# A two-layer decoder on one core: attention outputs scaled in place by transposed reciprocals

## The chip, the cores and the metric

The kernel is one program on 1 core of a Trainium2 chip. The metric is the device time in microseconds (us). Engines are named as the profile names them: PE (matmuls, with PEld for its weight loads), DVE (vector), ACT (activations), POOL (GpSimd) and SP (DMA issues).

## The reference

The input x is 64 batches x 128 tokens x 256 features, float32; ctx has the same shape. Six blocks follow one another, each added to x:

```python
x = x + mamba(layernorm(x))                       # state space scan
x = x + attention16(layernorm(x), ctx, ctx)       # 16 heads of 16, rotary, output projection
x = x + recurrence(layernorm(x))                  # 64 steps over the batches, gated, tanh output
x = x + self_attention(rmsnorm(x) * g)            # 16 query heads, 4 key heads, s + s @ w_o
x = x + wide_attention(layernorm(x), ctx, ctx)    # one head of 256
x = x + experts(layernorm(x))                     # top 2 of 8, and a shared expert
```

The change lies in the two 16-head attentions. For each head of 16 features they are

```python
attn_w = softmax(q @ k.T * scale, axis=-1)        # 1/4 in the cross attention, 1/16 in the self attention
out = attn_w @ v                                  # 128 tokens x 16 features a head
```

The cross attention ends with `out @ Wo + bo`; the self attention adds both `s` and `s @ w_o` to x.

## The kernel before

Four batches make a group of T = 512 tokens (G = 4), and there are NG = 16 groups. x stays in 16 tiles `X[g]`. There are four stages, one after the other: mamba; "work2" with the cross attention and the recurrence; "work3" with the self attention, the wide attention and the routing; and the experts, who work on rows that the routing has scattered to memory (`xs`). The text calls them stages 1 to 4.

Within a stage the work is written as generators, and `run(tasks)` sets their order: every generator has a turn at which it starts, and in each turn every active one advances to its next `yield`. In stages 2 and 3 the inputs of group g start at turn 16g, its recurrence at 16g + 42, its wide attention and routing (`cross_and_route`) at 16g + 43. The attention of batch b is two units, c = 0 and 1, of 8 heads each, that start at turn 16g + 16 + 4b + 2c: one unit every two turns, 8 units a group, 128 a stage, 256 in all. Each engine then executes its own instructions in the order in which they were issued; a scheduler fills in the semaphore waits. [...]

One unit, `heads`:

- POOL builds `kbd` (L284), the keys of four heads on a block diagonal, and PE multiplies the queries with it into `s` (L236; a float32 matmul is two records in the profile).
- DVE takes the maximum of every row and head (L241) and multiplies it with -scale (L242).
- ACT computes eight exponentials, one a head, with that maximum as bias (L245), into one tile `e`.
- PE transposes the eight (L250) into one tile `pt`; ACT copies the first half of it to `eT` (L252) and DVE the second (L253).
- PE multiplies `eT` with the values (L261) into `av`. The tile `v` has 16 columns of values and 16 of ones for each head, so that `av` has the weighted values in 16 rows and the sum of the exponentials in 16 others.

After the second unit of a batch ACT copies `av` (L267), PE transposes it with four transposes (`pa`, L272), DVE takes the reciprocals of the sums (L275) and multiplies the values with them (L277); two more transposes (`po`, L291, in `rows_T`) and an ACT copy (L293) bring the result back into the form that the output projection wants (L557 in the cross attention, L698 in the self attention). DVE adds that to x (L560, L701). The self attention has POOL add the outputs themselves to x (L690). POOL fills the columns of ones with a MEMSET for every batch (L533) or group (L669).

What stands around it: `norm` (bn statistics on DVE, L172; a power on POOL, L163; the scaling on DVE, L189) and `transposed` (PE, `pt_ln`, L200; ACT L202, DVE L204) before each projection (L211, L219); the rotary products (L512, L514, L519); the recurrence (L593, L598); the wide attention's exponentials, which are written with `accum_out` (L741), so that ACT also reads out the sum of a row with an instruction of its own; the routing's scatters by POOL (L842), eight for each group, of rows `xnr`. The first units of stage 3 are fed through a single tile `xo` that SP loads and POOL and ACT prepare (L643 to L645).

## Time and profile before

| | |
|---|---|
| Runs, us | 3532.44, 3531.86, 3532.04: median 3532.04 |
| The profiled execution | 3483.77 us, its span 3482.0 us |
| Stage 1 | 0 to about 787 us |
| Stage 2 | to about 1990; the last unit's maximum at 1924 |
| Stage 3 | to about 3075; the last unit's maximum at 2981, the last L701 at 3000.8 |
| Stage 4 | to the end |
| PE, DVE, ACT, POOL busy | 3176.3, 2273.2, 1471.3, 1302.8 us |
| L245, exponentials | 2048, 383 ns each |
| L241, maxima / L242, their scaling | 256 of 1213 ns / 256 of 333 ns |
| L250, transposes of e | 2048, 302 ns each from issue to end |
| mean granted clock of TensorE | 0.948 |

Times within a profile are microseconds from the start of its span. A group's row in the profile gives its busy time in all, the mean of one in ns, and after the bar the idle time of the engine just before these instructions with what ended most of it. Busy time is the union of records that overlap, so that a mean can be longer than the distance from one instruction to the next.

### The profile page before, as it was taken

How to read it: one execution, taken by the hardware profiler on the slowest of the kernel's cores; microseconds unless marked ns; L12 is line 12 of the kernel's file. 1: busy time of each engine (PE TensorE's matmuls, PEld its weight loads, DVE VectorE, ACT ScalarE, POOL GpSimd, SP SyncE). 2: the span in 40 equal slices, each digit the busy share in tenths (PEclk: the TensorE clock that was granted, in tenths of full speed). 3: DMA queues.
4: the chain of work that ended last, by engine and by line, in shares of the span. 5: the costliest groups of instructions: out<-in, count | busy, mean ns of one | idle time of the engine just before them, and what ended most of it. 6: DMA issues, size and time to landing. Idle time of an engine off the chain costs nothing.

```text
span 3482.0 us, 48744 instructions
## 1 busy us (share of the span) xinstructions
PE 3176.3 (91%) x17486; PEld 2033.9 (58%) x17486; DVE 2273.2 (65%) x5498; ACT 1471.3 (42%) x3781; POOL 1302.8 (37%) x1290
## 2 busy tenths in 40 slices
PE   7899999998999999999999767999999999779989
PEld 4555555554666666666666633556566655468845
DVE  7999889965565556655565344777777777543355
ACT  3333333334545555455545234555555555213301
POOL 2444444455332323332332064233333333223276
PEclk9999999999999999999999878999998999789999
DMA  9980000001000000000000011101010101157655
GB/s 312 343 283 1 1 1 1 1 14 30 13 19 13 19 13 13 14 18 19 13 13 7 34 50 41 37 32 42 32 43 32 42 31 43 60 167 227 200 182 180
DMA packets 170658, 229.48 MB, mean 66 GB/s; under 512 B 19504, under 2 KB 142896, under 8 KB 170416
## 3 DMA queue, kind: packets, MB, share of 16 engines
q1 hardware_dynamic: 152448, 180.19, 16.0%
q0 software_dynamic: 17968, 46.18, 4.3%
q8 instruction: 138, 2.26, 0.3%
q14 instruction: 104, 0.85, 0.1%
HBM read 113.71 MB, written 127.93 MB: 69 GB/s over the span
## 4 chain that ended last, share of the span: by engine, by line
PE 62%; DVE 24%; POOL 6%; ACT 4%; DMA 2%; issue 2%; ACTq 0%; DVEq 0%; POOLq 0%; SPq 0%
PE proj L211 17%; PE pt L250 7%; PE s L236 6%; PE pu L593 5%; DVE acc L333 4%; DVE xn L189 4%; PE pgu L1019 4%; PE pv L219 3%; PE pt_ln L200 2%; PE av L261 2%; DVE mx L241 2%; PE pd L1028 2%; PE pxo L219 2%; PE pd L1079 1%; PE po L439 1%
## 5 line engine op out<-in xcount | busy, mean ns | idle before, releaser
L245 ACT ACTIVATE e<-s,mx 128x128 f32<-128x128 f32 x2048 | 555.9, 383 | 479.6 <-DVE mx L242 390.0
L284 POOL TENSOR_TENSOR kbd<-kT,consts 128x512 f32<-128x512 f32 x192 | 202.9, 1057 | 682.3 <-PE s L236 674.0
L253 DVE COPY eT<-pt 128x512 f32<-128x512 f32 x256 | 176.0, 687 | 392.7 <-ACT eT L252 391.7
L250 PE MATMUL pt<-consts,e 128*128 128x128 f32 x2048 | 362.5, 302 | 64.4 <-ACT e L245 62.6
L250 PEld LDWEIGHTS pt<-consts,e 128*128 128x128 f32 x2048 | 258.5, 148 | 180.8 <-ACT e L245 124.5
L211 PE MATMUL proj<-xnT,win 128*128 128x512 f32 x640 | 308.1, 621 | 48.9 <-DVE xc L323 45.0
L241 DVE TENSOR_REDUCE mx<-s 128x8 f32<-128x1024 f32 x256 | 310.5, 1213 | 10.0 <-PE s L236 9.9
L236 PE MATMUL s<-kbd,qT 64*128 64x512 f32 x1024 | 311.1, 686 | 1.5 <-POOL kbd L284 1.5
L252 ACT COPY eT<-pt 128x512 f32<-128x512 f32 x256 | 153.0, 598 | 191.7 <-PE pt L250 190.5
L211 PEld LDWEIGHTS proj<-xnT,win 128*128 128x128 f32 x640 | 119.9, 197 | 192.6 <-issue 112.6
L842 POOL DMA_INDIRECT xs<-xnr,r_rows x128 | 126.6, 989 | 271.5 <-DMA xs<-xnr,r_rows 183.8
L333 DVE SCALAR_TENSOR_TENSOR acc<-proj,convw,acc 128x508 f32<-128x508 f32 (+2 forms) x288 | 209.2, 730 | 7.7 <-ACT acc L329 6.2
L593 PEld LDWEIGHTS pu<-c,fu 128*128 128x128 f32 x1536 | 184.8, 196 | 24.9 <-issue 18.9
L593 PE MATMUL pu<-c,fu 128*128 128x128 f32 x1536 | 187.4, 280 | 8.9 <-DVE c L609 8.9
L392 POOL TENSOR_TENSOR ua<-consts,dt 128x1024 f32<-128x1024 f32 x64 | 121.9, 1906 | 179.7 <-DVE dt L366 150.6
L261 PE MATMUL av<-eT,v 128*32 128x128 f32 (+1 forms) x3072 | 174.5, 328 | 10.0 <-DVE eT L253 9.8
L211 PE MATMUL proj<-xnT,fx 128*128 128x512 f32 x384 | 173.4, 601 | 10.1 <-DVE v L534 9.6
L200 PE MATMUL pt_ln<-consts,xn 128*128 128x128 f32 x640 | 125.6, 316 | 61.5 <-DVE xn L189 39.5
L163 POOL TENSOR_TENSOR ln_rstd<-ln_ve,neghalf 128x4 f32<-128x4 f32 x96 | 98.0, 1021 | 210.4 <-DVE ln_ve L176 158.8
L189 DVE TENSOR_SCALAR xn<-x,ln_mv,ln_rstd 128x256 f32<-128x256 f32 x256 | 142.0, 600 | 40.4 <-POOL ln_rstd L163 40.4
L598 DVE TENSOR_TENSOR xg<-pu,xg 128x512 f32<-128x512 f32 (+1 forms) x128 | 71.4, 558 | 131.6 <-PE pu L593 131.6
L172 DVE BATCH_NORM_STATS2 ln_st<-x 128x6 f32<-128x256 f32 x384 | 146.3, 406 | 13.2 <-DMA x<-in_x_dram 6.2
(266 smaller groups left out, 6508.5 us busy)
## 6 DMA issues: line engine op xcount, KB each, us to landing
xs<-zeros SPq DMA_DIRECT2D x64, 1024.0 KB, 11.1
xs<-xs SPq DMA_DIRECT2D x71, 256.0 KB, 3.4
ys<-y SPq DMA_DIRECT2D x71, 256.0 KB, 2.3
ctxT<-in_ctxT_dram SPq DMA_DIRECT2D x32, 512.0 KB, 3.9
xo<-xo SPq DMA_DIRECT2D x32, 512.0 KB, 3.5
x<-in_x_dram SPq DMA_DIRECT2D x16, 512.0 KB, 8.9
xn<-xnT SPq DMA_DIRECT2D x16, 512.0 KB, 2.6
xnT<-xn SPq DMA_DIRECT2D x16, 512.0 KB, 4.6
```

The costliest lines, as they stand in the source:

```text
L189: nc.vector.tensor_scalar(xn[:, b, :], x[:, b, :], mv[:, b, 0:1], rstd[:, b:b + 1], ALU.subtract, ALU.mult)
L200: nc.tensor.transpose(pt[:, b * P:(b + 1) * P], xn[:, b, c * P:(c + 1) * P], ident)
L211: nc.tensor.matmul(o[:m, :], lhsT=w[:, k, m0:m0 + m], rhs=rhs[:, k, :], start=(k == 0), stop=(k == 1))
L236: nc.tensor.matmul(s[:, hf * 4:hf * 4 + 4, :], lhsT=q[rows], rhs=kb[rows, :, :], start=True, stop=True,)
L241: nc.vector.tensor_reduce(mx, s, AX.X, ALU.max)
L245: nc.scalar.activation(e[:, h, :], s[:, h, :], AF.Exp, bias=mx[:, h:h + 1], scale=scale)
L250: nc.tensor.transpose(pt[:, h, :], e[:, h, :], ident)
L253: nc.vector.tensor_copy(eT[:, 4:8, :], pt[:, 4:8, :])
L261: nc.tensor.matmul(av[j * 32:j * 32 + 32, place, :], lhsT=vals, rhs=eT[:, which, :], start=True, stop=True,)
L284: nc.gpsimd.tensor_tensor(out=kb, in0=mid(k, 4), in1=last(head, P), op=ALU.mult)
L333: nc.vector.scalar_tensor_tensor(acc[:, :, k:], pv[:, :, :P - k], convw[:, c, 3 - k:4 - k], acc[:, :, k:], ALU.mult, ALU.add,)
L593: nc.tensor.matmul(pu[:, i, :], lhsT=fu[:, k, c * P:(c + 1) * P], rhs=c2[:, k, :], start=(k == 0), stop=(k == 1),)
```

## The change

Nine edits, all in the two attentions and in what feeds them:

1. Tiles that two engines fill or that are read in halves become separate tiles: `xnT`, `qT` and `kT` of the cross attention, `e`, `eT`, `pt` (tags pt0 and pt1[...]), and `xg`.
2. The factor -scale moves into the queries: POOL multiplies `xwq` and `xbq` with -0.25 and `lwq` with -1/16 once, and ACT writes `ym`, `yu` and `ymb` of the wide attention with -1/16. DVE then takes the minimum, and the exponential has scale -1. L242 and its sister L737 go.
3. The exponentials of `heads` get an `accum_out` into `den`, 128 tokens x 16 heads.
4. Per batch DVE takes the reciprocal of `den`, an ACT copy spreads it to 16 columns a head (`rd`, 128x256), PE transposes that with two transposes (`prd`), and ACT copies them out (`prs`).
5. DVE multiplies the first two columns of tiles of `av`, as they lie in PSUM, with `prs` and has `oT`. The copy `avs`, the four transposes `pa`, L277, and the transposes `po` with their copy go.
6. The values lie in three (stage 3: two) lasting tiles, whose 32 columns from 16 to 48 are zero from the start: even and odd heads accumulate into the same 32 rows of `av`. The columns of ones and their MEMSETs go. In the self attention a unit has eight products of 128 columns in place of four of 256.
7. The self attention adds the identity to the diagonal blocks of `lwo` once, and POOL's L690 goes.
8. The tail of a batch has four yields fewer, and the recurrence and `cross_and_route` start four turns earlier, at 16g + 38 and 16g + 39.
9. The routing stores its transposed rows with two DMAs a group in place of one.

```diff
@@ -155,6 +155,8 @@
+    for w in (xwq, xbq):
+        nc.gpsimd.tensor_scalar_mul(w, w, -0.25)
...
@@ -193,23 +195,26 @@
     def transposed(work, ps, xn, bufs=2):
-        xnT = work.tile([P, 2, T], F32, tag="xnT", name="xnT", bufs=bufs)
+        xnT = [work.tile([P, T], F32, tag=f"xnT{c}", name=f"xnT{c}", bufs=bufs) for c in range(2)]
         for c in range(2):
             pt = ps.tile([P, T], F32, tag="mm", name="pt_ln")
             for b in range(G):
                 nc.tensor.transpose(pt[:, b * P:(b + 1) * P], xn[:, b, c * P:(c + 1) * P], ident)
             if c == 0:
-                nc.scalar.copy(xnT[:, c, :], pt)
+                nc.scalar.copy(xnT[c], pt)
             else:
-                nc.vector.tensor_copy(xnT[:, c, :], pt)
+                nc.vector.tensor_copy(xnT[c], pt)
         return xnT
+    def halves(t):
+        return [t[:, c, :] for c in range(2)]
...
@@ -237,61 +241,79 @@
                 s[:, hf * 4:hf * 4 + 4, :], lhsT=q[rows], rhs=kb[rows, :, :],
                 start=True, stop=True,
             )
         mx = work.tile([P, 8], F32, tag="mx", name="mx", bufs=2)
-        nc.vector.tensor_reduce(mx, s, AX.X, ALU.max)
-        nc.vector.tensor_scalar(mx, mx, -scale, None, ALU.mult)
-        e = work.tile([P, 8, P], F32, tag="e", name="e", bufs=2)
+        nc.vector.tensor_reduce(mx, s, AX.X, ALU.min)
+        e, eT = (
+            [work.tile([P, 4, P], F32, tag=f"{n}{i}", name=f"{n}{i}", bufs=2) for i in range(2)]
+            for n in ("e", "eT")
+        )
+        if c == 0:
+            state[b, "den"] = work.tile([P, 16], F32, tag="den", name="den", bufs=4)
+        den = state[b, "den"]
         for h in range(8):
-            nc.scalar.activation(e[:, h, :], s[:, h, :], AF.Exp, bias=mx[:, h:h + 1], scale=scale)
-        yield
-        yield
-        pt = ps.tile([P, 8, P], F32, tag="pt", name="pt")
-        for h in range(8):
-            nc.tensor.transpose(pt[:, h, :], e[:, h, :], ident)
-        eT = work.tile([P, 8, P], F32, tag="eT", name="eT", bufs=2)
-        nc.scalar.copy(eT[:, 0:4, :], pt[:, 0:4, :])
-        nc.vector.tensor_copy(eT[:, 4:8, :], pt[:, 4:8, :])
-        yield
+            nc.scalar.activation(
+                e[h // 4][:, h % 4, :], s[:, h, :], AF.Exp, bias=mx[:, h:h + 1], scale=-1.0,
+                accum_out=den[:, c * 8 + h:c * 8 + h + 1],
+            )
+        yield
+        yield
+        for i in range(2):
+            pt = ps.tile([P, 4, P], F32, tag=f"pt{i}", name=f"pt{i}")
+            for h in range(4):
+                nc.tensor.transpose(pt[:, h, :], e[i][:, h, :], ident)
+            if i == 0:
+                nc.scalar.copy(eT[i], pt)
+            else:
+                nc.vector.tensor_copy(eT[i], pt)
+        if c == 1:
+            nc.vector.reciprocal(den, den)
+            rd = work.tile([P, 16, 16], F32, tag="rd", name="rd", bufs=2)
+            nc.scalar.copy(rd, last(den, 16))
+        yield
+        if c == 1:
+            pr = ps.tile([P, T], F32, tag="mm", name="prd")
+            for k in range(2):
+                nc.tensor.transpose(
+                    pr[:, k * P:(k + 1) * P],
+                    rd[:, 8 * k:8 * k + 8, :].rearrange("p h e -> p (h e)"), ident,
+                )
+            prs = work.tile([P, 2, P], F32, tag="prs", name="prs", bufs=2)
+            nc.scalar.copy(prs.rearrange("p c t -> p (c t)"), pr[:, :D])
         yield
         if c == 0:
             state[b] = ps.tile([P, 4, P], F32, tag="av", name="av")
         av = state[b]
-        for vals, which, j, place in vh(c):
-            nc.tensor.matmul(
-                av[j * 32:j * 32 + 32, place, :], lhsT=vals, rhs=eT[:, which, :],
-                start=True, stop=True,
-            )
+        for odd in range(2):
+            for j in range(4):
+                h = 2 * j + odd
+                nc.tensor.matmul(
+                    av[j * 32:j * 32 + 32, c, :], lhsT=vh(h), rhs=eT[h // 4][:, h % 4, :],
+                    start=(odd == 0), stop=(odd == 1),
+                )
         if c == 1:
-            avs = work.tile([P, 4, P], F32, tag="avs", name="avs", bufs=2)
-            nc.scalar.copy(avs, av)
-            yield
-            yield
-            pa = ps.tile([P, T], F32, tag="mm", name="pa")
-            for g4 in range(4):
-                nc.tensor.transpose(pa[:, g4 * P:(g4 + 1) * P], avs[:, g4, :], ident)
-            pav = pa.rearrange("p (h e) -> p h e", e=32)
-            rd = work.tile([P, 16], F32, tag="rd", name="rd", bufs=2)
-            nc.vector.reciprocal(rd, pav[:, :, 16])
-            o = work.tile([P, D], F32, tag="o", name="o", bufs=2)
-            nc.vector.tensor_tensor(
-                o.rearrange("p (h e) -> p h e", e=16), pav[:, :, 0:16], last(rd, 16), ALU.mult
-            )
-            state[b] = o
+            yield
+            oT = work.tile([P, 2, P], F32, tag="oT", name="oT", bufs=2)
+            nc.vector.tensor_tensor(oT, av[:, 0:2, :], prs, ALU.mult)
+            state[b] = oT
+    def values_of(work, n, i):
+        v = work.tile([P, n, 64], F32, tag=f"v{i}", name=f"v{i}")
+        nc.gpsimd.memset(v[:, :, 16:48], 0.0)
+        return v
+    def pairs(v):
+        return v.rearrange("p n (f e) -> p n f e", e=16)[:, :, 0:4:3, :]
     def block_diagonal(work, k):
         kb = work.tile([P, 4, P], F32, tag="kbd", name="kbd", bufs=2)
         nc.gpsimd.tensor_tensor(out=kb, in0=mid(k, 4), in1=last(head, P), op=ALU.mult)
         return kb
-    def rows_T(work, ps, o):
-        po = ps.tile([P, T], F32, tag="mm", name="po")
-        for c in range(2):
-            nc.tensor.transpose(po[:, c * P:(c + 1) * P], o[:, c * P:(c + 1) * P], ident)
-        oT = work.tile([P, 2, P], F32, tag="oT", name="oT", bufs=2)
-        nc.scalar.copy(oT.rearrange("p c t -> p (c t)"), po[:, :D])
-        return oT
     XS = scratch.tile([8 * CAP + TS, D], F32, tag="xs", name="xs")
...
@@ -480,6 +502,10 @@
+        wd = lwo[:, c, c * P:(c + 1) * P]
+        nc.gpsimd.tensor_tensor(out=wd, in0=wd, in1=ident, op=ALU.add)
+    nc.gpsimd.tensor_scalar_mul(lwq, lwq, -1.0 / 16)
...
@@ -510,17 +536,17 @@
-                tv = t[:, c, :].rearrange("p (b t) -> p b t", b=G)
+                tv = ts[c].rearrange("p (b t) -> p b t", b=G)
-            got[g, tag] = t
-            yield
-            yield
-        got[g, "c"] = cT
+            got[g, tag] = ts
+            yield
+            yield
+        got[g, "c"] = halves(cT)
...
@@ -529,28 +555,21 @@
             if c == 0:
                 pv = ps.tile([P, T], F32, tag="mm", name="pv")
                 project_rows(pv[:, :D], got[g, "c"], xwv, b)
-                v = work.tile([P, 16, 32], F32, tag="v", name="v", bufs=3)
-                nc.gpsimd.memset(v[:, :, 16:32], 1.0)
+                v = got["v"][(g * G + b) % 3]
                 nc.vector.tensor_tensor(
-                    v[:, :, 0:16], pv[:, :D].rearrange("p (h e) -> p h e", e=16),
-                    xbv.rearrange("p (h e) -> p h e", e=16), ALU.add,
+                    pairs(v), pv[:, :D].rearrange("p (n f e) -> p n f e", f=2, e=16),
+                    xbv.rearrange("p (n f e) -> p n f e", f=2, e=16), ALU.add,
                 )
                 got[g, b, "v"] = v
             v = got[g, b, "v"]
-            return lambda c: [
-                (v[:, h, :], h % 8, h % 4, h // 4) for h in range(8 * c, 8 * c + 8)
-            ]
+            return lambda h: v[:, 4 * c + h // 2, h % 2 * 32:h % 2 * 32 + 32]
         yield from heads(
-            work, ps, b, c, got, got[g, "qT"][:, c, tb],
-            lambda: block_diagonal(work, got[g, "kT"][:, c, tb]), values, 0.25,
+            work, ps, b, c, got, got[g, "qT"][c][:, tb],
+            lambda: block_diagonal(work, got[g, "kT"][c][:, tb]), values,
         )
         if c == 1:
-            o = got[b]
-            yield
-            yield
-            oT = rows_T(work, ps, o)
-            yield
+            oT = got[b]
             yield
             pr = ps.tile([P, T], F32, tag="mm", name="pr")
             for k in range(2):
...
@@ -569,12 +588,14 @@
-        xg = work.tile([P, 6, T], F32, tag="xg", name="xg")
+        xgs = [work.tile([P, n, T], F32, tag=f"xg{n}", name=f"xg{n}") for n in (4, 2)]
-                nc.scalar.activation(xg[:, c, :], pp, AF.Identity, bias=fb[:, c:c + 1])
+                nc.scalar.activation(
+                    xgs[c // 4][:, c % 4, :], pp, AF.Identity, bias=fb[:, c:c + 1]
+                )
...
@@ -613,10 +633,10 @@
-        ps = PsumPool(psp, {"mm": 3, "s": 1, "pt": 1, "av": 1})
-        got = {"c2": c2}
+        ps = PsumPool(psp, {"mm": 3, "s": 1, "pt0": 1, "pt1": 1, "av": 1})
+        got = {"c2": c2, "v": [values_of(work, 8, i) for i in range(3)]}
-        tasks += [(16 * g + 42, recurrence(g, work, ps, got)) for g in range(NG)]
+        tasks += [(16 * g + 38, recurrence(g, work, ps, got)) for g in range(NG)]
...
@@ -665,9 +685,8 @@
-        v = work.tile([P, G * 4, 32], F32, tag="v", name="v", bufs=2)
-        nc.gpsimd.memset(v[:, :, 16:32], 1.0)
-        nc.scalar.copy(v[:, :, 0:16], pv[:, :D].rearrange("p (h e) -> p h e", e=16))
+        v = got["v"][g % 2]
+        nc.scalar.copy(pairs(v), pv[:, :D].rearrange("p (n f e) -> p n f e", f=2, e=16))
...
@@ -681,17 +700,10 @@
         yield from heads(
             work, ps, ("o", b), c, got, qT[:, c, tb], keys,
-            lambda: lambda c: [
-                (v[:, b * 4 + j, :], slice(j, 8, 4), j, slice(2 * c, 2 * c + 2)) for j in range(4)
-            ], 1.0 / 16,
+            lambda: lambda h: v[:, b * 2 + h % 4 // 2, h % 2 * 32:h % 2 * 32 + 32],
         )
         if c == 1:
-            o = got["o", b]
-            nc.gpsimd.tensor_tensor(out=X[g][:, b, :], in0=X[g][:, b, :], in1=o, op=ALU.add)
-            yield
-            yield
-            oT = rows_T(work, ps, o)
-            yield
+            oT = got["o", b]
             yield
             pr = ps.tile([P, T], F32, tag="mm", name="pr")
             for k in range(2):
...
@@ -727,19 +740,18 @@
-                    s[:, b, :], lhsT=qT[:, k, tb], rhs=cT[:, k, tb], start=(k == 0), stop=(k == 1)
+                    s[:, b, :], lhsT=qT[:, k, tb], rhs=cT[k][:, tb], start=(k == 0), stop=(k == 1)
-        nc.vector.tensor_reduce(mx, s, AX.X, ALU.max)
+        nc.vector.tensor_reduce(mx, s, AX.X, ALU.min)
-        nc.vector.tensor_tensor(mx, qb, mx, ALU.subtract)
-        nc.vector.tensor_scalar(mx, mx, 1.0 / 16, None, ALU.mult)
+        nc.vector.tensor_tensor(mx, mx, qb, ALU.subtract)
-                e[:, b, :], s[:, b, :], AF.Exp, bias=mx[:, b:b + 1], scale=1.0 / 16,
+                e[:, b, :], s[:, b, :], AF.Exp, bias=mx[:, b:b + 1], scale=-1.0,
...
@@ -779,7 +791,8 @@
-        nc.sync.dma_start(out=XN[g], in_=xnT)
+        for c in range(2):
+            nc.sync.dma_start(out=XN[g][:, c, :], in_=xnT[c])
...
@@ -849,7 +862,7 @@
-        ps = PsumPool(psp, {"mm": 3, "s": 1, "pt": 1, "av": 1})
+        ps = PsumPool(psp, {"mm": 3, "s": 1, "pt0": 1, "pt1": 1, "av": 1})
...
@@ -869,8 +882,9 @@
-        nc.scalar.copy(yu, pb[:, :D + 1])
-        nc.scalar.copy(ymb, pb[:, D + 1:D + 3])
+        nc.scalar.mul(yu, pb[:, :D + 1], -1.0 / 16)
+        nc.scalar.mul(ymb, pb[:, D + 1:D + 3], -1.0 / 16)
@@ -878,7 +892,7 @@
-            nc.scalar.copy(ym[:, c, :], pw[:, :D])
+            nc.scalar.mul(ym[:, c, :], pw[:, :D], -1.0 / 16)
...
@@ -886,9 +900,9 @@
-        got = {"full": base}
+        got = {"full": base, "v": [values_of(work, G * 2, i) for i in range(2)]}
-        tasks += [(16 * g + 43, cross_and_route(g, work, ps, got)) for g in range(NG)]
+        tasks += [(16 * g + 39, cross_and_route(g, work, ps, got)) for g in range(NG)]
...
```

More of the change, by code (lines that the diff above doesn't have):

```diff
@@ L211, in project @@
             nc.tensor.matmul(
-                o[:m, :], lhsT=w[:, k, m0:m0 + m], rhs=rhs[:, k, :], start=(k == 0), stop=(k == 1)
+                o[:m, :], lhsT=w[:, k, m0:m0 + m], rhs=rhs[k], start=(k == 0), stop=(k == 1)
             )
@@ L219, in project_rows, with heads @@
             nc.tensor.matmul(
-                dst, lhsT=lhsT[:, k, b * P:(b + 1) * P], rhs=w[:, k, :] if m is None else w[:, k, m],
+                dst, lhsT=lhsT[k][:, b * P:(b + 1) * P], rhs=w[:, k, :] if m is None else w[:, k, m],
                 start=(k == 0), stop=(k == 1),
             )
-    def heads(work, ps, b, c, state, q, kbd, v, scale):
+    def heads(work, ps, b, c, state, q, kbd, v):
         kb, vh = kbd(), v()
@@ L499, in cross_inputs @@
         yield
-        for w, bias, src, tag in ((xwq, xbq, xnT, "qT"), (xwk, xbk, cT, "kT")):
-            t = work.tile([P, 2, T], F32, tag=tag, name=tag, bufs=2)
+        for w, bias, src, tag in ((xwq, xbq, xnT, "qT"), (xwk, xbk, halves(cT), "kT")):
+            ts = [work.tile([P, T], F32, tag=f"{tag}{c}", name=f"{tag}{c}", bufs=2) for c in range(2)]
             raws = []
@@ L596, in recurrence @@
                         )
-                pre = xg[:, c0:c0 + n, tb]
+                pre = xgs[c0 // 4][:, :, tb]
                 nc.vector.tensor_tensor(pre, pu[:, 0:n, :], pre, ALU.add)
@@ L603, in recurrence @@
             new = work.tile([P, 2, P], F32, tag="new", name="new")
-            nc.vector.scalar_tensor_tensor(kept, xg[:, 0:2, tb], 1.0, c2, ALU.add, ALU.mult)
-            nc.vector.scalar_tensor_tensor(
-                new, xg[:, 2:4, tb], 1.0, xg[:, 4:6, tb], ALU.add, ALU.mult
-            )
+            xa, xb = (t[:, :, tb] for t in xgs)
+            nc.vector.scalar_tensor_tensor(kept, xa[:, 0:2, :], 1.0, c2, ALU.add, ALU.mult)
+            nc.vector.scalar_tensor_tensor(new, xa[:, 2:4, :], 1.0, xb, ALU.add, ALU.mult)
             got["c2"] = const.tile([P, 2, P], F32, tag="c2", name="c2", bufs=2)
@@ L703, in wide_attention @@
     def wide_attention(g, work, ps):
-        cT = load_ctx(work, g, 1)
+        ctx_tile = load_ctx(work, g, 1)
+        cT = halves(ctx_tile)
         xn = norm(work, g)
@@ L1068, in shared_expert @@
             hs = [
-                gated(project(ps, msg, c * P, P, xnT), project(ps, msu, c * P, P, xnT), f"hs{c}")
+                gated(
+                    project(ps, msg, c * P, P, halves(xnT)),
+                    project(ps, msu, c * P, P, halves(xnT)), f"hs{c}",
+                )
                 for c in range(2)
```

## The prediction

> **What bounds the kernel now.** I read the page's engine table and clock row first, then busy time by stretch of the span, then the groups of instructions with their idle times, and last the order of single instructions in time. Page, parts 1 and 2:
>
> ```profile
> PE 3176.3 (91%) x17486; PEld 2033.9 (58%) x17486; DVE 2273.2 (65%) x5498; ACT 1471.3 (42%) x3781; POOL 1302.8 (37%) x1290
> ...
> PEclk9999999999999999999999878999998999789999
> ```
>
> PE leads over the span, but the change touches two stages only. Busy time of each engine in those two, where their attention units run without a break (columns: stretch, length, then busy us and counts of PE, PEld, DVE, ACT, POOL, granted clock, DMA share, GB/s):
>
> ```profile
> 813.00:1924.00 1111.00, 1068.71 (x6950) 690.75 (x6949) 649.67 (x1370) 575.78 (x1589) 361.81 (x350) 0.99 0.04 15
> 2170.00:2981.00 811.00, 776.62 (x4523) 483.94 (x4516) 599.63 (x1800) 427.63 (x1352) 262.67 (x285) 0.93 0.11 37
> ```
>
> PE is 96% busy in both, ACT 52 to 53%, DVE 58% in stage 2 and 74% in stage 3. Busy is not work, though: the groups show what PE's records hold.
>
> ```profile
> L245 ACT ACTIVATE e<-s,mx 128x128 f32<-128x128 f32 x2048 | 555.9, 383 | 479.6 <-DVE mx L242 390.0
> ...
> L253 DVE COPY eT<-pt 128x512 f32<-128x512 f32 x256 | 176.0, 687 | 392.7 <-ACT eT L252 391.7
> L250 PE MATMUL pt<-consts,e 128*128 128x128 f32 x2048 | 362.5, 302 | 64.4 <-ACT e L245 62.6
> L250 PEld LDWEIGHTS pt<-consts,e 128*128 128x128 f32 x2048 | 258.5, 148 | 180.8 <-ACT e L245 124.5
> ```
>
> A transpose of e follows the one before in 0.109 us when nothing holds it, yet these occupy 362.5/2048 = 0.177 us each and have another 181 us of idle in front of their loads: PE waits for the exponentials. Unit by unit (256 of them, 8 heads each) the chain is: last score matmul, L241 (1.213 us), L242, eight L245 (2.17 us together), L250. While it runs PE does other work, a filler of 2.6 to 9 us. Past what the filler covers, the eight transposes come 0.48 us late per unit in stage 2 and 1.0 us in stage 3. From one steady group to the next (8 units) it is 73.0 us in stage 2 (1142.94 to 1215.94) and 57.9 us in stage 3 (2413.30 to 2471.03 to 2529.18). So stage 2 is bound mostly by PE's work, stage 3 by PE's work in half of its units and the chain in the others.
>
> **What the Trainium skill says.** "TensorE: Matmul & The Clock Gate", Part 1, says that TensorE falls to half clock after an idle window of about 3.4 us. The trace has granted clock 0.93 in stage 3 and 0.99 in stage 2, with cold stretches of 3.4 to 10.2 us about once a group in stage 3: it agrees, so added idle time can cost twice. "ScalarE: Activation LUTs", in its cost section, puts an activation with a per-partition bias at about 280 ns + 0.833 ns an element, some 93 ns of it hidden back to back: about 294 ns for 128 elements as an estimate. Here one is 383 ns and eight take 2.17 us, a pitch near 0.26: the trace decides.
>
> **The change part by part.**
>
> *PE work.* Per batch (128 in all) four L272 and two L291 transposes go and two of rd come. Two cancel. Four L272 take 0.53 us a batch, so 68 us less for PE (79.5 busy). Counting each group's matmuls in the changed program's order at pitches from the trace (0.43 us for 512 columns, 0.216 for 256, 0.112 for 128), PE's work per group goes from 66.3 to 64.5 us in stage 2 and 49.2 to 47.5 in stage 3. Weighted sums stay at their 0.58 us per unit.
>
> *The chain.* L242 goes: 85.2 us over 256, 0.33 each; from L241's end to the first exponential it is 0.81 us on average now and needs about 0.15. Against it, each exponential now reads its accumulator. The nearest rows are L741's four: ACT 2524.27, 2524.61, 2524.95, 2525.30, a pitch of 0.34, with the last read ending at 2525.83:
>
> ```profile
> 2524.27 0.42 ACT L741 ACTIVATE e<-s,mx 128x128 f32<-128x128 f32 x1
> 2524.52 0.26 ACT L741 ACTIVATION_READ_ACCUMULATOR e<-s,mx 128x1 f32 x1
> 2524.61 0.42 ACT L741 ACTIVATE e<-s,mx 128x128 f32<-128x128 f32 x1
> ```
>
> Eight are 2.74 to 2.93 us: 0.56 to 0.76 more a unit, 143 to 195 us more of ACT, and the transposes wait for the read. Per batch ACT sheds L267 (0.622) and L293 (0.398) and takes two 256-column copies (about 0.4 each): 0.2 back. The bare chain goes from about 4.2 us to 4.6. But it does not run bare: L241 starts 0.69 (stage 2) and 0.80 us (stage 3) after the scores where 0.26 is possible, mostly right behind L253, which waits 391.7 us in all for ACT's half of the same eT. Divided tiles end that wait. Measured means now: 0.75 + 1.21 + 0.81 + 2.17 = 4.9; after: 0.3 + 1.21 + 0.15 + 2.85 + 0.1 = 4.6. Bounds for the chain: +0.4 (nothing of the queueing goes) and -0.4.
>
> *Stage 2.* PE's work, -1.8 us a group, counts nearly whole. pt_ln has waited 20.6 us for DVE's kT (L514) over 14 groups, 1.5 each; with divided tiles I take half of that. Total -2.5 a group, x16 = **-40**. Ends: -1.2 (the fillers grow uneven in the new order: one of 12.6 us, others of 3.4) and -5 (the times from a unit's last score to its last transpose add up to 61.3 in a measured group, fillers plus transposes to 57.2, and most of these 4.1 us also goes).
>
> *Stage 3.* PE's fillers change from 3.07, 3.5, 5.1, 4.54, 2.59, 3.55, 4.24, 7.13 us to 3.5, 1.0, 2.6, 5.8, 3.45, 4.9, 4.2, 6.69 (units of a group in order). From the last score to the last transpose is measured now as 4.27, 4.74, 6.03, 5.43, 5.91, 5.9, 5.17, 8.56 = 46.0. After it is the larger of filler + 0.8 and the 4.6 chain (4.7 with its last transpose): 4.7, 4.7, 4.7, 6.6, 4.7, 5.7, 5.0, 7.5 = 43.6, or -2.4. Against that, four turns fewer put the route's normalization beside the next self-attention's: ahead of one unit's minimum DVE now has about four xnr (0.423 each) and four BN_STATS (0.406), 3.3 us, and the filler there is one of the short ones. Net +0.9; and POOL has route's rstd behind the eight scatters of the group before:
>
> ```profile
> 2514.69 0.99 POOL L842 DMA_INDIRECT xs<-xnr,r_rows  x1 [0.93 <-DMA xs<-xnr,r_rows]
> 2517.41 0.96 POOL L842 DMA_INDIRECT xs<-xnr,r_rows  x1 [1.73 <-DMA xs<-xnr,r_rows]
> 2520.07 0.96 POOL L842 DMA_INDIRECT xs<-xnr,r_rows  x1 [1.70 <-DMA xs<-xnr,r_rows]
> ```
>
> Their pitch is 2.66 us, each waiting for the DMA of the last: eight need 21 to 24 us. Before, 27.2 us lay between their rows and that rstd; after, 19 to 22. That is 0 to 3 us late, on the unit just named; I take 0.1, since only the excess over the 3.3 us already counted reaches PE. So +1.0, over 14 steady groups **+14**. Ends: -2.4 and +4.3.
>
> *Tails.* From the last L241 to the last X add is 21 us in stage 2 and 19.8 in stage 3 (2981 to 3000.8). Four turns fewer, without L267 (0.62), L272 (0.53), L275 and L277 (0.25 + 0.41) and the handoffs between them in that order: about 7 each, **-14** (-6 to -16).
>
> *The rest.* Nothing else is on the path. L690 (46.7 us), L533 and L669 (24.9) leave POOL, a third busy. The weight scalings on POOL at the start (1.5 to 4 us) lie in stage 1, which PE and DVE fill. Sixteen more DMA issues for XN on SP come with DMA 11% busy; nobody awaits them before stage 4. The copy rd, its transposes and prs run while the weighted sums' operands are fetched; were they late, L300's product waits, then only the output projection. Together +2 (0 to 5). The first fourteen units of stage 3 wait for a single xo buffer, unchanged.
>
> Sum: -40 + 14 - 14 + 2 = -38. The profiled execution takes 3483.77 us (span 3482.0), so 3446; the median of the runs, 3532.04, stands 48.3 us above the profiled one, and I keep that offset: **3494**.
>
> **Rivals.** *Slower: normalization and scatters collide in stage 3.* The unit's minimum waits for xnr, those for POOL's rstd, that for the scatters; PE has 1 to 3 us of filler there. At +4.3 a group x14 = +60, with stage 2 at its low end (-1.2 x16 = -19), tails -8 and +4 for the rest: +37, 3569. It decides from about +4 a group in stage 3. For it: DVE is 74% busy there and the pitch of the scatters is fixed. Against it: before, the last scatter ends some 2 us ahead of that rstd, so the collision starts only past that slack. *The exponentials' reads bind.* If the chain is 0.4 longer wherever the transposes wait, about 60 of 112 units in stage 3 lose 0.4, +24, and stage 2 keeps its low end: near -15, 3517. *No change:* stage 3 gives back exactly what stage 2 and the tails bring, about 3532. *Much faster:* both stages at their good ends, -5 x16 and -2.4 x14 with the tails, -125, or about 3410; it needs every wait gone, so I give it little.
>
> **How the numbers follow.** My case with its shading toward more or less (the second rival is its upper edge): 0.48, of it 0.44 beyond 0.2%. The collision: 0.39. No change proper: 0.05. Much faster: 0.08. A measurement of this kernel can tell about 0.2%, 7 us. So faster 0.52, within 0.2% 0.09, slower 0.39. The range holds both main cases, 3440 to 3585; my own case alone would be 3465 to 3520.
>
> **What would show it.** Right: group period near 70.5 us in stage 2 and at or under 59 in stage 3; DVE's eT copy no longer waiting for ACT's; eight exponentials with reads in 2.7 to 2.9 us; the minimum starting about 0.3 us after the scores. Wrong: a stage 3 period over 61 us with xn or xnr waiting on POOL; stage 2 still at 72; or PE waiting at pt for the reads more than the 181 us now.

## The result, and the profile after

The changed kernel takes 3498.71 us (median of 4 runs, 3492.24 to 3506.03) where the kernel before takes 3531.95 beside it: a ratio of 0.9908 (95% interval 0.9887 to 0.9928), 33 us less. The forecast was 3494 us, and faster.

The two profiled executions say something else at first sight: 3483.77 us before and 3496.45 after. They must not be subtracted, because stage 4, which the change leaves alone, runs differently on different chips. The issues of the output stores on SP, kernel before, then after (start, length, instruction):

```profile
3323.73 12.09 SPq L1059 DMA_DIRECT2D out_dram<-x  x2
3344.92 9.43 SPq L1059 DMA_DIRECT2D out_dram<-x  x2
```

```profile
3291.81 11.84 SPq L1073 DMA_DIRECT2D out_dram<-x  x2
3312.53 27.27 SPq L1073 DMA_DIRECT2D out_dram<-x  x2
```

A row with x2 holds two stores and the time from the first to the second. Before, the stores follow one another every 9 to 12 us; after, one pair lies 27 us apart, and from the last X add of stage 3 to the last DVE instruction it is 477 us before against 520 after. A later comparison settles whose gaps these are (run b_again). So I read both traces up to that last X add (L701, now L713): 3001.2 us before, 2970.8 after, **30.4 us less**, which agrees with the timed 33.

The page after, parts 1 and 2:

```profile
PE 3168.8 (91%) x17998; PEld 1996.2 (57%) x17998; DVE 2202.7 (63%) x5226; ACT 1615.6 (46%) x5829; POOL 1236.4 (35%) x1156
...
PEclk9999999998999999999999779999999998799989
```

Busy time in stage 2 (first to last minimum) and in stage 3, columns as before:

```profile
817.00:1905.00 1088.00, 1059.50 (x6757) 665.93 (x6755) 608.56 (x1257) 649.55 (x2610) 343.23 (x290) 0.99 0.05 15
2143.00:2960.00 817.00, 773.75 (x5158) 471.60 (x5158) 583.50 (x1668) 485.30 (x2220) 219.28 (x219) 0.96 0.11 37
```

ACT rose from 52% to 60% busy; PE is 97 and 95% busy and its work is less. The groups:

```profile
L256 ACT ACTIVATE e<-s,mx 128x128 f32<-128x128 f32 x2048 | 719.4, 379 | 415.4 <-DVE mx L246 415.3
...
L265 PE MATMUL pt<-consts,e 128*128 128x128 f32 x2048 | 401.7, 296 | 75.0 <-ACT e L256 69.0
L256 ACT ACTIVATION_READ_ACCUMULATOR e<-s,mx 128x1 f32 x2048 | 448.4, 219 | 0.0
L265 PEld LDWEIGHTS pt<-consts,e 128*128 128x128 f32 x2048 | 253.8, 143 | 231.5 <-ACT e L256 191.4
...
L269 DVE COPY eT<-pt 128x512 f32<-128x512 f32 x256 | 173.4, 677 | 136.5 <-PE pt L265 135.5
```

The transposes wait for ACT longer than before (PEld's idle time ahead of them is 231.5 us against 180.8), and DVE's copy of eT no longer waits for ACT's. In ACT's timeline an exponential with its read (the ACTIVATION_READ_ACCUMULATOR) has the pitch that L741 showed, 0.34 us, and eight take 2.81 from the first start to the end of the last exponential:

```profile
2467.96 0.37 ACT L256 ACTIVATE e<-s,mx 128x128 f32<-128x128 f32 x1 [0.53 <-DVE mx L246]
2468.22 0.19 ACT L256 ACTIVATION_READ_ACCUMULATOR e<-s,mx 128x1 f32 x1
2468.31 0.36 ACT L256 ACTIVATE e<-s,mx 128x128 f32<-128x128 f32 x1
```

Where the time went, from the starts of the minima (maxima) and the last X adds of each stage:

| stretch, us | before | after | difference | forecast |
|---|---|---|---|---|
| start to the first maximum of stage 2 | 812.8 | 817.1 | +4.3 | +2 |
| stage 2, first to last maximum | 1110.9 | 1088.0 | -22.9 | -40 |
| its tail, to the last X add | 21.7 | 11.3 | -10.4 | -7 |
| to the first maximum of stage 3 | 86.4 | 86.8 | +0.4 | 0 |
| stage 3, first 24 units | 207.6 | 199.4 | -8.2 | 0 |
| stage 3, the rest | 741.5 | 757.0 | +15.5 | +14 |
| its tail, to the last X add | 20.3 | 11.2 | -9.1 | -7 |

The group period is 70.3 us in stage 2 (from 73.0) and 58.8 in stage 3 (from 58.0).

### The profile page after: what moved, and what is told of

Its sections match the earlier page's. It is cut to its first block, busy times and chain, and to the rows that moved or that the text cites. A ratio compares the mean times of both kernels' runs of the same rounds, so it can differ in the third digit from the quotient of the medians.

```text
span 3494.7 us, 51286 instructions
## 1 busy us (share of the span) xinstructions
PE 3168.8 (91%) x17998; PEld 1996.2 (57%) x17998; DVE 2202.7 (63%) x5226; ACT 1615.6 (46%) x5829; POOL 1236.4 (35%) x1156
## 5 line engine op out<-in xcount | busy, mean ns | idle before, releaser
L256 ACT ACTIVATE e<-s,mx 128x128 f32<-128x128 f32 x2048 | 719.4, 379 | 415.4 <-DVE mx L246 415.3
L265 PE MATMUL pt<-consts,e 128*128 128x128 f32 x2048 | 401.7, 296 | 75.0 <-ACT e L256 69.0
L256 ACT ACTIVATION_READ_ACCUMULATOR e<-s,mx 128x1 f32 x2048 | 448.4, 219 | 0.0
L265 PEld LDWEIGHTS pt<-consts,e 128*128 128x128 f32 x2048 | 253.8, 143 | 231.5 <-ACT e L256 191.4
L293 PE MATMUL av<-eT,v 128*32 128x128 f32 x4096 | 178.9, 286 | 5.6 <-DVE eT L269 5.4
L300 DVE TENSOR_TENSOR oT<-av,prs 128x256 f32<-128x256 f32 x128 | 54.0, 422 | 200.1 <-ACT xo L602 113.0
L1057 POOL DMA_INDIRECT ys<-ys,t_yrow x128 | 123.4, 964 | 92.6 <-DVE x L1069 43.3
```

Source lines behind the costliest of these rows:

```text
L256: nc.scalar.activation(e[h // 4][:, h % 4, :], s[:, h, :], AF.Exp, bias=mx[:, h:h + 1], scale=-1.0, accum_out=den[:, c * 8 + h:c * 8 + h + 1],
L265: nc.tensor.transpose(pt[:, h, :], e[i][:, h, :], ident)
L293: nc.tensor.matmul(av[j * 32:j * 32 + 32, c, :], lhsT=vh(h), rhs=eT[h // 4][:, h % 4, :], start=(odd == 0), stop=(odd == 1),)
```

## The experiments

Runs whose name begins with b change the kernel before, those with a the kernel after. The ratio is to the kernel before on the same chip; "to X" is the last X add of stage 3 in the profile, which leaves stage 4 out. A period is the time from one group's first minimum (maximum) to the next one's: in stage 2 the median of the steady groups, in stage 3, where groups alternate, their mean. Unchanged kernels repeat "to X" within 3 us (before) and 7 us (after), and the periods within 0.1 us. Clock is the mean granted TensorE clock of stage 3 after its first 24 units.

| run | ratio (95%) | to X | period, stage 2 | stage 3 | clock |
|---|---|---|---|---|---|
| before / b_again | 0.9998 (0.9988 to 1.0007) | 3001.2 / 3004.2 | 73.0 / 73.0 | 58.0 / 58.0 | 0.93 / 0.92 |
| b_fold | 0.9911 (0.9895 to 0.9928) | 2971.0 | 71.7 | 58.4 | 0.93 |
| b_split | 0.9986 (0.9979 to 0.9993) | 2991.1 | 72.1 | 57.9 | 0.93 |
| b_foldsplit | 0.9952 (0.9934 to 0.9970) | 2983.7 | 71.9 | 59.0 | 0.93 |
| b_fsreads | 1.0136 (1.0118 to 1.0154) | 3047.1 | 71.3 | 63.3 | 0.89 |
| after / a_again | 0.9911 (0.9891 to 0.9932) | 2970.8 / 2977.6 | 70.3 / 70.3 | 58.8 / 58.8 | 0.96 / 0.95 |
| a_scale | 1.0271 (1.0252 to 1.0290) | 3088.7 | 75.1 | 61.8 | 0.95 |
| a_joined | 1.0676 (1.0658 to 1.0693) | 3242.1 | 76.8 | 69.9 | 0.88 |
| a_joined2 | 0.9957 (0.9943 to 0.9972) | 2988.3 | 71.7 | 59.0 | 0.97 |
| a_noread | 0.9774 (0.9758 to 0.9791) | 2926.7 | 69.7 | 57.5 | 0.97 |
| a_pe4 | 0.9887 (0.9871 to 0.9904) | 2965.3 | 70.9 | 57.8 | 0.96 |
| a_43 | 0.9908 (0.9884 to 0.9932) | 2967.5 | 70.3 | 58.0 | 0.92 |

A warning on all of them: the scheduler orders each engine's instructions anew for every edit, so a run measures its edit together with the order that it brings.

**Does PE's work count? (a_pe4)**

```diff
+            for k in (2, 3, 2, 3):
+                nc.tensor.transpose(
+                    pr[:, k * P:(k + 1) * P],
+                    rd[:, 8 * k - 16:8 * k - 8, :].rearrange("p h e -> p (h e)"), ident,
                 )
```

> The kernel after, with four more transposes of rd per batch into the unused half of prd (each half is written twice). Nothing reads them; they put back the PE work of the four L272. Theory A (stage 2 is bound by PE's work, stage 3 by the chain of exponentials in most units): stage 2's group period goes from 70.3 to about 72.1 us (4 x 0.44), stage 3's from 58.5 to at most 59.3; about +35 us in all. Rival B (stage 2 gained by its shorter waits, not by the transposes that went): both periods move by under 0.4 us, under +10 in all.

Stage 2 went up by 0.6 us a group, not 1.8, and stage 3 came down by 1.0: in all 6 to 12 us less to X than the two runs of the kernel after. Neither theory holds as written. About a third of the transposes' time counts in stage 2, and nothing shows in stage 3, where the unit of the norms, whose minimum started 1.4 to 2.5 us after the scores, had a new order in which it starts 0.2 to 1.3 us after them. PE's 97% busy is not 97% work: 1.76 us of work more a group cost 0.6 in stage 2.

**What L242 cost (a_scale, b_fold)**

```diff
         nc.vector.tensor_reduce(mx, s, AX.X, ALU.min)
+        nc.vector.tensor_scalar(mx, mx, 1.0, None, ALU.mult)
```

> The kernel after, with one more DVE instruction between the minimum and the exponentials (mx times 1.0), as L242 stood there before. Theory A: stage 2 +0.3 us a group at most, stage 3 +1 to +2 (8 units, three quarters of them waiting, 0.2 to 0.3 each): +15 to +35 us in all. Rival B: stage 2 +1.5 or more a group. A second rival, that DVE's queue and not the chain is what L242 cost (0.81 us from its maximum to the first exponential): the delay comes back as 0.5 us or more a unit, and stage 3 loses 3 us a group.

It came out at +118 us to X (+111 against the repetition), +4.8 a group in stage 2 and +3.1 in stage 3: far over theory A, as the second rival said, and more. From the minimum to the first exponential it was 0.80 us on average in stage 2, as before the change (0.81), against 0.04 in the kernel after. DVE's timeline of one unit of a_scale:

```profile
1336.77 1.21 DVE L246 TENSOR_REDUCE mx<-s 128x8 f32<-128x1024 f32 x1
1337.90 0.68 DVE L541 TENSOR_TENSOR qT<-rot,consts 128x512 f32<-128x512 f32 x1
1338.50 0.76 DVE L247 TENSOR_SCALAR mx<-mx 128x8 f32<-128x8 f32 x1
```

The same in the kernel before:

```profile
1178.85 1.21 DVE L241 TENSOR_REDUCE mx<-s 128x8 f32<-128x1024 f32 x1
1179.98 0.68 DVE L514 TENSOR_TENSOR kT<-rot,consts 128x512 f32<-128x512 f32 x1
1180.58 0.76 DVE L242 TENSOR_SCALAR mx<-mx 128x8 f32<-128x8 f32 x1
```

And in the kernel after, where no second step is left that could be held up:

```profile
1232.47 1.21 DVE L246 TENSOR_REDUCE mx<-s 128x8 f32<-128x1024 f32 x1
1233.61 1.27 DVE L540 TENSOR_TENSOR qT<-rot,consts 128x512 f32<-128x512 f32 x2
```

A product for another group stands between the maximum and its scaling, and the exponentials wait for both. This is no single case: in the kernel before, other DVE work stands between L241 and L242 in 178 of the 256 units, 102 of these in stage 2. Removing that step alone:

```diff
-        nc.vector.tensor_reduce(mx, s, AX.X, ALU.max)
-        nc.vector.tensor_scalar(mx, mx, -scale, None, ALU.mult)
+        nc.vector.tensor_reduce(mx, s, AX.X, ALU.min)
...
+    for w in (xwq, xbq):
+        nc.gpsimd.tensor_scalar_mul(w, w, -0.25)
...
+    nc.gpsimd.tensor_scalar_mul(lwq, lwq, -1.0 / 16)
```

> The kernel before with the second edit alone (in the 16-head attentions): -scale goes into xwq, xbq and lwq, the minimum is taken, L242 is gone. Theory A2 (what L242 costs is not its 0.2 us but its place in DVE's order: other work gets between it and the maximum, and with it the exponentials come 0.5 to 0.8 us later): stage 2's period falls from 73.0 to 69 to 71.5, stage 3's from 58.0 to 55.5 to 57; -50 to -90 us in all. Rival (the saving shows only together with the divided tiles, since the minimum still starts late behind DVE's copy of eT): under 1 us a group in both, -30 at most.

Measured: -32 us, at 0.9911 the same as the whole change. The size is near the rival's, its reason is not: no divided tile was needed. Stage 2 gained 1.3 us a group, 22 us in all, where the mean delay from the maximum to the first exponential fell from 0.8 to 0.1 us. In steady stage 3 it fell from 0.7 to 0.1, and yet the period did not fall (58.4). But the first 24 units of stage 3 took 190.1 us in place of 207.6, and there the delay had another cause. In the kernel before, the exponentials of 13 of the first 16 units follow directly on ACT's L644, the preparation of xo, which waits for POOL. One of them:

```profile
2071.56 0.17 DVE L242 TENSOR_SCALAR mx<-mx 128x8 f32<-128x8 f32 x1
2071.99 2.34 POOL L643 TENSOR_TENSOR xo<-xo,hc 128x1024 f32<-128x1024 f32 x1 [3.91 <-DMA xo<-xo]
2074.36 1.06 ACT L644 ACTIVATE xo<-xo 128x1024 f32<-128x1024 f32 x1 [2.88 <-POOL xo L643]
2075.32 2.15 ACT L245 ACTIVATE e<-s,mx 128x128 f32<-128x128 f32 x8
```

In b_fold 8 of these 16 do, and the mean delay falls from 3.1 to 1.8 us. So this part of the 32 us comes with a new order on ACT that the edit brought along, not with DVE's queue; no run separates the two. That the same step costs 111 to 118 us in the order of the kernel after, where the reads have made the chain longer, shows too that it has no price of its own.

**The divided tiles (a_joined, a_joined2, b_split, b_foldsplit)**

```diff
+        e8, eT8 = (work.tile([P, 8, P], F32, tag=n, name=n, bufs=2) for n in ("e", "eT"))
...
+        pt8 = ps.tile([P, 8, P], F32, tag="pt", name="pt")
```

> The kernel after, with e, eT and pt of a unit as one tile each again (the other divided tiles stay). Theory A: DVE's half of eT waits for ACT's again, some 300 us in all, and holds up the next minimum: stage 2 +0.5 to +1 us a group, stage 3 +1 to +3; +25 to +60 in all. Rival C (that wait of DVE is hidden, since DVE has 40% of its time free): under 0.3 a group in both, under +8 in all.

+271 us to X, over every expectation, and from a wait that I had built myself: with one tile `pt` the second four transposes came after ACT's copy of the first four. In steady stage 2 the fifth transpose started 1.5 us after the fourth on average, late in all 112 units; in the kernel after it was 0.15. In stage 3 it was 2.5 against 0.5. It says what undivided tiles do in the new order of statements, not what they did before. With all eight transposes ahead of both copies:

```diff
-            for h in range(4):
-                nc.tensor.transpose(pt[:, h, :], e[i][:, h, :], ident)
...
+        pt = ps.tile([P, 8, P], F32, tag="pt", name="pt")
+        for h in range(8):
+            nc.tensor.transpose(pt[:, h, :], e8[:, h, :], ident)
+        nc.scalar.copy(eT[0], pt[:, 0:4, :])
+        nc.vector.tensor_copy(eT[1], pt[:, 4:8, :])
```

> The kernel after with e, eT and pt as one tile each, and all eight transposes issued ahead of both copies, as in the kernel before. The run a_joined had the second four transposes behind ACT's copy of the first four, in the same tile, which cost 2 us a unit in itself. Theory: stage 2's period 70.3 goes to 70.8 to 72, stage 3's 58.8 to 59.5 to 62, +20 to +60 us. Rival (DVE's wait for ACT's copy is hidden): within 10 us of the kernel after.

+18 us against the first profile of the kernel after, +11 against its repetition, and a ratio of 0.9957 against 0.9908 and 0.9911: some 16 us. That is a little under the theory's range and over the rival's, and it lies mostly in stage 2 (+1.4 a group).

The same tiles divided in the kernel before (e, eT, pt, with two products of 128 columns where the self attention had one of 256):

```diff
-        pt = ps.tile([P, 8, P], F32, tag="pt", name="pt")
...
+        for i in range(2):
+            pt = ps.tile([P, 4, P], F32, tag=f"pt{i}", name=f"pt{i}")
```

> The kernel before with e, eT and pt divided alone (in the self attention the products of 256 columns become two of 128). Theory: DVE's wait for ACT's half of eT, 391.7 us, falls below 150 us, the maximum starts 0.3 us sooner, and each group gains 0.5 to 1.5 us: -15 to -45 us in all. Rival (that wait is hidden): within 10 us of the kernel before.

The ratio 0.9986 is 5 us, 2 to 7 by its interval: the rival's range. (The profiled execution, 10 to 13 us less to X, is one of the faster of 20.) DVE's wait at eT did not go; in the run's waits (us in all, times, longest) it is for PE in place of ACT:

```profile
ACT e L248 <- DVE mx L242: 469.8, 181, 5.7
DVE eT L258 <- PE pt L254: 296.7, 90, 7.5
```

So 297 of the 391.7 us that I had read as a cost of the joint tile are still waited, for PE, and the rest was worth 5 us: DVE had little in its order that was more urgent.

Both edits together:

> The kernel before with the scale in the queries and with e, eT and pt divided, but with the old normalization (ones among the values, avs, pa, po) and no reads. Theory: the two gains add up (-32 and -4 to -10 us on the chip of the last comparison), so that it is 35 to 45 us under the kernel before and at or a little under the kernel after: accumulator reads cost the kernel after what its shorter tails and fewer transposes bring. Rival: the maximum now comes early enough with either, and it is as b_fold, -32.

-17 us by the ratio (0.9952), less than b_fold's -32, on another chip. Both theories fail: the gains don't add. Stage 2's period is nearly that of b_fold, stage 3's is 0.6 us longer, and its first 24 units take 196.7 us, 6.6 more. Why dividing the tiles costs here what it brought there stays open.

**The accumulator reads, and the last rung (a_noread, b_fsreads)**

The kernel after without the reads; the softmax is then not divided by its sums:

```diff
-                accum_out=den[:, c * 8 + h:c * 8 + h + 1],
...
-            nc.vector.reciprocal(den, den)
+            nc.vector.reciprocal(den, state["dc"])
```

> The kernel after without accum_out in the 16-head attentions: the 2048 reads of the accumulator go, and the reciprocals are taken of a constant, so the softmax is not divided by its sums. Theory A: eight exponentials fall from 2.81 to 2.17 us; stage 2 loses 0 to 0.5 us a group, stage 3 2 to 4 (86 of 112 units wait for the exponentials there, 0.64 each): -30 to -65 in all. Rival D (in stage 3 the norms ahead of one minimum set the time, the reads don't): stage 3 under -1 a group, under -15 in all.

-44 us to X as theory A has it in sum: eight exponentials take 2.18 us, stage 2 gives 0.6 a group, stage 3's period 1.3 (less than the 2 expected, near rival D), its first 24 units 8. So the reads, with the wait of the reciprocal for them, take back more than the whole change earns.

And b_foldsplit with reads whose sums nothing uses; against b_foldsplit (arguments left out at "..."):

```diff
-            nc.scalar.activation(e[h // 4][:, h % 4, :], ..., scale=-1.0)
+            nc.scalar.activation(e[h // 4][:, h % 4, :], ..., scale=-1.0, accum_out=den[:, h:h + 1])
```

> The last rung between the two kernels: before + scale in the queries + divided e, eT, pt + accum_out in the 16-head exponentials, whose sums nothing uses (the old normalization with ones, avs, pa and po stays). Measured to the last X add, so that stage 4 stays out: before 3001 to 3004, with the first two edits 2984, after 2971 to 2978. Taking the reads out of the kernel after brought 44 us. Theory: they cost as much here, so that this kernel stands at 3020 to 3035, and the output scaled in place, with its shorter tails and fewer transposes, is worth 45 to 60 us over it. Rival (the reads cost only where the new order is crowded): 2984 to 2995, and the output scaled in place is worth under 20, no more than the tails.

3047: the reads cost 63 us here, and the output scaled in place is worth 70 to 76 over it, both more than expected. (That last rung holds all that is left of the change: the output path, the shorter tails with their turns, and the other divided tiles.) From rung to rung the time to X is 3001 to 3004 before, 2971 with the scale folded, 2984 with the tiles divided too, 3047 with the reads, 2971 to 2978 after. Stage 2 shows nothing of the cost (71.3); it is in stage 3, mostly in the steady groups, 59.0 to 63.3 us each. There the clock fell. One group of b_fsreads, windows of 3.4 us on PE (columns: window, length, PE busy and count, granted clock, DMA share, GB/s):

```profile
2496.25:2499.65 3.40, 3.40 (x36) 1.00 0.05 19
2499.65:2503.05 3.40, 2.20 (x31) 1.00 0.00 0
2503.05:2506.45 3.40, 3.36 (x10) 0.60 0.02 5
2506.45:2509.85 3.40, 2.53 (x21) 0.50 0.01 2
2509.85:2513.25 3.40, 3.40 (x15) 0.50 0.00 0
```

One group of the kernel after:

```profile
2433.90:2437.30 3.40, 2.04 (x26) 1.00 0.04 16
2437.30:2440.70 3.40, 2.05 (x11) 1.00 0.38 141
2440.70:2444.10 3.40, 3.40 (x12) 0.51 0.00 0
2444.10:2447.50 3.40, 3.40 (x37) 0.99 0.02 5
```

In both, a stretch in which PE stood for a third of the time or more comes shortly before the half clock, which lasts three windows in the one kernel and one in the other. It is no rule: over stage 3 of the kernel after, in steps of 3.41 us at which its clock changes, 10 windows at full clock in which PE was busy for 27 to 91% were followed by half clock, and 16 in which it was busy for 51 to 75% were not. The clock records of all these runs hold only full and half clock, so a mean clock c over a period P means a loss of (1 - c) x P in clock pulses: 4.1 us a group in b_foldsplit (0.93 of 59.0), 7.0 in b_fsreads (0.89 of 63.3), 2.4 in the kernel after (0.96 of 58.8). Of the +4.3 us that the reads bring, 2.9 would then be clock; of the -4.5 that the output scaled in place brings, all. That is arithmetic with clocks given to a hundredth (0.3 us each way), not an experiment: what would be needed is a run in which only the clock differs, and none does that. The run a_43 below speaks against it: its clock is 0.92, which by the same arithmetic loses 4.6 us a group, 2.2 more than the kernel after, and its period is 0.7 us shorter. So what the 63 us consist of stays open.

**The turn of the routing (a_43)**

```diff
-        tasks += [(16 * g + 39, cross_and_route(g, work, ps, got)) for g in range(NG)]
+        tasks += [(16 * g + 43, cross_and_route(g, work, ps, got)) for g in range(NG)]
```

> The kernel after, with cross_and_route starting at turn 16g + 43 again (4 turns later), all else the same. Theory (the route's and the next group's norms meet ahead of one minimum in stage 3, which starts 2.5 us late there in two groups of three and costs that unit some 2 to 3 us): stage 3's period falls from 58.8 to 55.5 to 57.5, -15 to -45 us in all, stage 2 unchanged. Rival (another unit takes the wait, whatever the turn): within 10 us.

The rival's range: 3 us less to X, the same ratio as after. Stage 3's period falls by 0.7 us, its first 24 units take 4 us more, and its tail grows from 11.2 to 12.5. The wait moved to another unit, as the rival said: the minimum of a group's first unit now starts 0.05 us after the scores in place of 1.9, that of its fourth 2.5 in place of 1.3.

**Whose are stage 4's gaps? (b_again, a_again)**

> The kernel before, unchanged. Its profiled execution took 3483.77 us where its other runs took 3530 to 3532, and in it the last output stores of stage 4 went out every 10 us, where all profiles of the kernel after and of its variants have gaps of 15 to 27 us among them (514 to 524 us from the last X add to the end, against 477). If the gaps are the rule for this kernel too, this profile shows them and has a span of 3525 to 3531; if they come from the change, it is 3482 again.

> The kernel after, unchanged, on a chip together with the two kernels below. On the chip where the kernel before takes 3485 us (its stage 4 without the gaps between output stores), I expect 3446 to 3456: the stages up to the last X add come 30 to 35 us sooner, as in the first profile, and stage 4 takes 477 to 480. If the change itself brought the gaps of stage 4, it would be 3490 there.

The kernel before, unchanged, took 3485.3 us on that chip (median of 32 runs), and its profile has no gaps: 478 us from the last X add, as have all kernels of that comparison, with parts of the change (b_fold 476, b_split 479, and a_joined2, 476, which stores the routing's rows in two parts as the kernel after does). On three other chips it takes 3529 to 3532, and every profile from those has 514 to 529 us, b_foldsplit and b_fsreads among them, which leave stage 4 and its stores as before. a_again ran on one of those: 3500.67 beside 3531.26. Its expected 3446 to 3456 was for the other chip, and no run of the kernel after was made there. So the gaps go with the chip, and the two comparisons of the whole change, both on chips with gaps, agree (33 and 31 us). Each chip was used on one occasion, so that chip and occasion can't be told apart; but all 42 executions of the kernel before on the first took 3481 to 3491 us, and the 27 on those three 3523 to 3538. What holds the stores up isn't shown: SP waits for DVE (149.1 us in the kernel after), and for the longest pauses of DVE and ACT there (17.6 and 42.2 us) the trace names no releaser.

## Why the prediction was right, and where it was not

The total was right, 3494 for 3499, and so was the sign, which the prediction held for little more than even (0.52). That it came this close is in part luck, for errors cancelled: stage 2 brought 17 us less than its term, the tails and the first 24 units of stage 3 brought 14 more. The range, 3440 to 3585, held the slower case as well. Step by step:

- **Eight exponentials with reads, 2.74 to 2.93 us:** 2.81. Right, as was the pitch from L741.
- **L242:** the step "it is 0.81 us on average now and needs about 0.15" was right (0.04 in stage 2, 0.10 in steady stage 3). I had it as one term in a chain that the reads nearly bring back (4.9 before, 4.6 after). Alone it brings 32 us, as much as the whole change, and the reads take 44 to 63: two large terms, of which I had priced only a small difference.
- **Divided tiles end DVE's wait of 391.7 us:** the wait at ACT's copy ended, and with it some 5 us in the kernel before and 16 in the kernel after. The term that the minimum starts at 0.3 us after the scores was too good: it starts at 0.05 in most units, but at 0.56 on average in stage 2 and 0.72 in stage 3, where other DVE work stands in front in some units.
- **Stage 2, -2.5 a group:** -2.7 (70.3, forecast near 70.5). But "PE's work, -1.8 us a group, counts nearly whole" failed: a_pe4 puts back 1.76 and costs 0.6. The rest would then be shorter waits; which of them isn't shown. And "x16" was mis-sized: the first two intervals (48.6 to 49.8 and 62.5 to 68.0) and the last (71.3 to 73.5) grew, so that the stage gave 22.9 us and not 40.
- **Stage 3, +1.0 a group:** +0.8, and +15.5 over the steady part for +14. The unit that was named is there: the route's and the next group's norms lie ahead of its minimum, which starts 1.4 to 2.5 us after the scores, 2.5 in the group shown. (a_43, which starts the route four turns later again, leaves the ratio as it is and gains 3 to 10 us to X, so that this wait alone did not set the time.) DVE's timeline of the kernel after:

```profile
2434.70 0.42 DVE L174 BATCH_NORM_STATS2 ln_st<-x 128x6 f32<-128x256 f32 x1
2435.97 0.16 DVE L183 TENSOR_TENSOR ln_ms<-ln_rstd 128x4 f32<-128x4 f32 x1 [0.85 <-POOL ln_rstd L165]
2436.05 0.42 DVE L174 BATCH_NORM_STATS2 ln_st<-x 128x6 f32<-128x256 f32 x1
2436.39 1.21 DVE L246 TENSOR_REDUCE mx<-s 128x8 f32<-128x1024 f32 x1
```

  The rival's second half, the scatters holding up POOL, did not come: the power waits for DVE, not for a scatter.

```profile
2425.90 0.96 POOL L855 DMA_INDIRECT xs<-xnr,r_rows  x1 [1.71 <-DMA xs<-xnr,r_rows]
...
2434.93 1.01 POOL L165 TENSOR_TENSOR ln_rstd<-ln_ve,neghalf 128x4 f32<-128x4 f32 x1 [3.91 <-DVE ln_ve L178]
```

- **Tails, -14:** -19.5. The price per tail was 7 and is 9 to 10.
- **"The first fourteen units of stage 3 ... unchanged":** the first 24 units gained 8.2 us. Nothing in the prediction stood for that; b_fold, with the missing L242 and the order that it brings, gains 17.5 there. In the kernel after, 7 of the first 16 units' exponentials follow directly on ACT's preparation of xo, in place of 13.
- **"I keep that offset" of 48.3 us:** the step gave the right median for a reason that I did not know, the chip.
- **The clock, misread and left out:** "added idle time can cost twice" was said of the clock, from the Trainium skill's "TensorE: Matmul & The Clock Gate", Part 1, and then not priced. The page names an idle window of about 3.4 us, and the prediction took the trace to agree. It does not, and the measurement decides: ahead of 12 of the 13 half-clock stretches of steady stage 3 in the kernel before, the longest pause of PE within 3.4 us was 0.2 to 1.4 us, ahead of the other 2.15. Stage 3's clock went from 0.93 to 0.96, which by the arithmetic above is 1.7 us a group in the kernel's favour; a_43 shows that such a difference need not appear in the period.
- **Signs:** of the signs of being right, the last failed (the minimum at 0.3 us after the scores); of the signs of being wrong, one came: PE waits at pt for longer than 181 us, 231.5. The gain came in spite of it.
- **A sum:** the second rival's terms, +24 and -19 with -14 and +2 for the tails and the rest, give -7 and not -15, so that its 3517 should have been near 3525.

## What to carry to other kernels

Don't price a small instruction in the middle of a chain between engines by its length alone; look at what the scheduler puts in front of it. With 0.33 us of L242 the exponentials came 0.7 us later in stage 2, and taking it out brought as much as the whole change, about half of that in units where the order on another engine changed with it. A wait in the profile is not yet a cost; 392 us of it were worth 5 here. An edit can change an engine's order far from where it was made, so read where a gain lies before naming its cause. And before subtracting two profiles, subtract a stage that the change does not touch.

## What the hardware showed that I had not expected

- The same kernel took 3485 us on one chip and 3529 to 3532 on three others. By the profiles of this kernel and its variants the difference lies in stage 4 (476 to 479 us against 514 to 529), in its last 165 to 215 us, where output stores, gathers and loads overlap.
- The granted clock of TensorE was full or half and nothing between, in steps of 3.41 us, and half clock came without a long pause of PE: in the kernel before ahead of 12 of 13 stretches no pause was longer than 1.4 us. In the kernel after, PE's busy share in such a step did not foretell it (27 to 91% ahead of half clock, 51 to 75% in 16 steps without it). Nor did the idle time in sum: the mean clock of stage 3 lay between 0.88 and 0.97 over these kernels, and the kernel after, with more idle time at pt (231.5 us ahead of its loads), had a higher one than the kernel before (180.8). What does foretell it stays open.
